# Cross-attention with layer normalisation on one core: the order of all engines listed anew, low parts of the projections last, half of the q copies on ScalarE and half of the scales on VectorE

## The chip, the cores and the metric

The kernel runs on one core of a Trainium2 chip. The metric is the device time in microseconds of one execution. The core has five engines, each of which runs its instructions strictly in program order: TensorE (PE in the profile, with PEld for its weight loads), VectorE (DVE), ScalarE (ACT), GpSimd (POOL) and SyncE (SP), which here issues DMA transfers. A matmul reads SBUF and writes PSUM, which has eight banks of 128 partitions x 512 fp32.

## The reference

```python
qs = (x @ wq).reshape(4, 2048, 16, 32).transpose(0, 2, 1, 3)
ks = (ctx @ wk).reshape(4, 77, 16, 32).transpose(0, 2, 1, 3)
vs = (ctx @ wv).reshape(4, 77, 16, 32).transpose(0, 2, 1, 3)
scores = einsum('bhqd,bhkd->bhqk', qs, ks) / sqrt(32)
scores = where(mask, -inf, scores)            # mask over the 77 keys
attn = einsum('bhqk,bhkd->bhqd', softmax(scores), vs)
out = attn.transpose(0, 2, 1, 3).reshape(4, 2048, 512) @ wo + x
mu, var = mean(out, -1), mean((out - mu) ** 2, -1)
return (out - mu) / sqrt(var + 1e-5) * gamma + beta
```

x is (4, 2048, 512) in fp32, ctx (4, 77, 512). There are 16 heads of 32 columns.

## The kernel before, in words

The 8192 rows of x form 64 tiles t of 128 rows, 32 blocks b of 256 rows (two tiles) and 16 groups g of 512 rows (four tiles). The accuracy of fp32 is kept in the two projections by splitting both operands into a high part in a short format and a low part, the remainder (`xth`/`xtl`, `wqh`/`wql`, `AH`/`AL`, `woh`/`wol`). Each projection is then a sum of three products, high by high, high by low and low by high, over four chunks c of 128: 12 matmuls of 128x512.

The order of all work is one long string, `ORDER`. It is a list of words, each a letter with a number: the letter names a step, the number its tile, block or group, and the program is written word by word, so the string fixes the order on each engine. The words that matter here:

- `Q` on PE: q projection of a group for four heads (12 matmuls, L275). Four of them fill the q of a group. `q` is the copy of the result out of PSUM (L289).
- `S` on PE: scores of a tile (64 small matmuls in 32x64 pieces, L405), four banks. `T` on DVE: mask added and row maximum taken (`pbuf`, `nm`, L422). `e` on ACT: the exponential (L437). `r` on DVE: the reciprocal of the sum (L447). `n` on POOL: the normalising product (L452). `t` on DVE: the transpose into `B` (L473).
- `P`: one of twelve DMA transfers of a block that regroup `B` into `PT` (L484). Its suffix gives the queue: `s` SyncE, `g` GpSimd, `a` ScalarE. `V` on PE: the product with the values (32 matmuls, L498), which needs all twelve. Where `V` stands right behind an `S` on PE, the first matmul of the `S` already waits for them.
- `a` on ACT and `b` on DVE: high and low part of the result (`AH` L527, `AL` L531). `O` on PE: out projection of a tile (12 matmuls, L554).
- `x`, `+`, `s`: x row tile loaded, residual added (DVE L563), moments (DVE L577, L578). `v` on POOL: 1/sqrt(var + eps) and -mean/sqrt(...) as four small operations (`rn`, L583 to L586). `k` on ACT: the scale with bias (L592). `f` and `)` on POOL: gain and shift (L595, L598). `w`: the store.
- `g`, `i`, `j`: x transposed loaded, cast to the high part (ACT), split into the low part (POOL L269).

A run of matmuls of one word is called a visit. A full visit is `Q`, `O` or another with 128 rows and columns, against `S` and `V`, which use the array in smaller pieces; a change of kind is where a visit of one of the three kinds follows one of another.

`SLOTS` assigns buffers and PSUM banks to the values in the order in which they come, so a new order goes with new numbers. Where VectorE splits wv or wo (`F`, `G`), the next `j`, `n`, `f` or `)` on POOL is made to wait until VectorE is done with it (`shared` and `wait_for`).

Of the kernel before, what the change touches and what calls it, by code (L numbers as in the profile page):

```python
# [8 lines left out]
F32 = mybir.dt.float32  # L9
# [25 lines left out]
for b in range(4):  # L35
# [7 lines left out]
NPB = 3  # L43
KSCALE = 1.0 / HD**0.5
# [10 lines left out]
T5.0 e6.1 P1.2s P1.1s P1.8s j7 Q14 Z16.s P1.6s n4 t4 S7 Z2.s T7.3 e5.2 e6.3 e6.2 e7.3 T7.0 e7.0 T7.2 T5.3 T5.1 r6
P1.11s T7.1 e7.1 e7.2 q14 P1.10s P1.9s P1.7s P1.4s Q8 q8 Q11 q11 r7 Q13 n6 t6 e5.3 e5.1 e5.0 S9 T9.0 n7 T9.3 t7 r5 n5
V1 a1.1 a1.0 b1.0 x0 g8 i8 j8 g9 b1.1 T9.1 V0 a0.1 T9.2 Z8.s b0.1 x3 Z15.s O2 L1 i9 x2 S8 P3.6s P3.2s P3.8s j9 t5 e9.1
a0.0 b0.0 e9.2 e9.0 +2 T8.3 e8.3 T8.1 e8.1 =24.8 T8.0 e8.0 s2 T8.2 O3 +3 s3 q13 v1 P3.10s Z14.s P3.0s O0 P3.7s P3.9s
P3.1s Z4.s P3.5s e9.3 S10 T10.2 +0 Y1 Z13.s P3.4s x4 T10.3 e8.2 P3.11s P2.7s P2.8s P3.3s T10.1 e10.3 r9 k3 e10.1 T10.0
e10.0 e10.2 r8 n8 f3 P2.5s P2.6s n9 )3 Z5.s P2.4s O1 +1 Q15 q15 s1 t8 Q12 q12 S11 T11.2 T11.1 e11.2 T11.3 e11.3 k2 V3  # L60
S12 a3.0 a3.1 s0 v0 k0 P2.1s P2.9s f2 r10 n10 t9 P2.10s P2.3s P2.11s P2.0s P2.2s g11 b3.0 T12.2 Z9.s w3 e11.1 e12.2
i11 j11 b3.1 Z11.s x7 f0 P4.0s P4.1s P4.9s P4.5s P4.8s g10 x5 P4.3s Q18 T12.1 q18 T12.0 T12.3 e12.3 T11.0 e11.0 P4.6s
x6 P4.4s O7 +7 S13 t10 s7 r11 n11 T13.2 T13.3 V2 a2.0 T13.0 P4.11s T13.1 P4.10s P4.7s P4.2s a2.1 b2.1 t11 P5.5s )2 k1
f1 Q19 O6 P5.3s P5.2s P5.10s P5.4s e12.0 S14 T14.1 T14.3 e12.1 r12 n12 T14.0 T14.2 b2.0 +6 s6 P5.9s w2 g12 e13.2 P5.0s
# [31 lines left out]
+26 S37 T37.2 T37.1 x29 T37.0 b14.0 P16.0s P16.9s f22 )22 e35.1 i22 e35.3 f23 )23 i23 r35 n35 j22 s27 V15 s26 v13 t35
T37.3 w22 P16.1s e36.0 x28 e37.1 e36.3 e36.2 P16.3s Q43 q43 e37.2 e37.0 a15.1 e37.3 r36 O29 k26 S38 T38.2 T38.0 T38.3
T38.1 e38.1 e38.0 P16.5s P17.1s P17.2s P17.6s O28 +29 +28 s28 s29 P17.7s g24 n36 r37 t36 j23 b15.1 a15.0 b15.0 v14
P17.0s f26 Q41 q41 n37 e38.2 P17.10s P17.8s P17.4s k27 w23 x31 k28 Q42 q42 S39 T39.2 P17.5s w25 T39.1 T39.3 e38.3 f27
k29 i24 P17.11s V16 a16.0 t37 j24 e39.3 r38 b16.0 n38 x30 P17.3s P17.9s S40 T40.3 T40.1 T39.0 e40.3 e39.1 P18.10s  # L100
P18.11s P18.8s P18.3s x32 P18.2s )26 P18.1s P18.6s P18.9s x33 O30 +30 s30 T40.0 O31 +31 t38 Q47 T40.2 a16.1 e39.0
e39.2 r39 n39 f28 s31 v15 b16.1 e40.2 e40.0 f29 )29 )28 S41 T41.3 e40.1 e41.3 T41.2 t39 V17 g25 T41.0 a17.1 T41.1
e41.2 L3 P18.4s P18.7s Q45 r40 w26 P18.5s b17.1 P18.0s P19.6s g27 n40 w28 P19.8s q47 Q44 q44 k31 f31 k30 f30 a17.0 i25
j25 S42 T42.1 P19.0s P19.1s P19.7s O33 e41.1 e41.0 )27 T42.0 T42.2 T42.3 e42.3 b17.0 O32 r41 +33 e42.0 s33 t40 S43 +32
e42.2 P19.9s P19.10s T43.2 P19.3s x34 w29 T43.0 P19.11s P19.2s T43.3 g26 x35 P19.5s P19.4s e42.1 T43.1 r42 n41 n42 s32
v16 t41 e43.3 V18 a18.0 a18.1 Q46 Q50 )31 =48.8 e43.1 e43.0 q46 q45 P20.5s i27 j27 P20.3s S44 P20.1s P20.9s x38 w27
q50 b18.0 P20.10s P20.7s T44.1 T44.0 x37 w31 T44.2 t42 O34 k33 T44.3 f33 e43.2 i26 k32 e44.0 e44.1 S45 T45.0 r43
# [67 lines left out]
def xattn_layernorm(  # L175
# [625 lines left out]
```

## Time and profile before

| | us |
|---|---|
| three runs | 508.16, 508.02, 506.6 |
| median of the runs | 508.02 |
| span of the profiled execution | 506.2 |
| the median less that span | 1.8 |

The profile comes from one execution; its span runs from the first to the last instruction. Engine rows give busy time, share of the span and number of instructions. In rows of groups stands: line, engine, operation, result <- operands by their names in the kernel, partitions x elements, type and count, then busy time and mean ns of one, then the idle time of the engine just before them with what ended it.

### The profile page before, as it was taken

The numbers are of one execution on the slowest core, as the hardware profiler recorded it, in microseconds if no ns is written. First come the engines' busy times: TensorE is split into PE (matmuls) and PEld (weight loads), VectorE is DVE, ScalarE is ACT, GpSimd is POOL, SyncE is SP. The second block draws the span as 40 slices with busy tenths as digits, with TensorE's granted clock in tenths as the row PEclk, the third lists the DMA queues.
The fourth block names the chain that finished last, engine by engine and source line by source line (L and its number), as shares of the span: only waits on it lengthen the run. The fifth ranks groups of instructions, "written<-read, shape, count | busy, mean of one in ns | idle before, by whom it ended". The sixth has DMA issues, their size and how long they took to land.

```text
span 506.2 us, 20312 instructions
## 1 busy us (share of the span) xinstructions
PE 498.8 (99%) x6831; PEld 383.1 (76%) x6831; DVE 460.5 (91%) x2539; ACT 473.9 (94%) x2248; POOL 421.3 (83%) x387
## 2 busy tenths in 40 slices
PE   9999999999999999999999999999999999999995
PEld 6987778777777777777777777777777777877773
DVE  5799988999899999898898898998999999899997
ACT  6699999999999999999999999999999998999851
POOL 2666464789886798989989887999998999999896
PEclk9999999999999999999999999999999999999999
DMA  8957577889886796859887778877888769888746
GB/s 306 396 197 175 135 212 183 221 210 217 247 242 178 177 248 199 249 165 253 243 216 204 200 207 240 230 201 193 248 232 225 207 177 293 247 199 222 183 150 232
DMA packets 58782, 110.86 MB, mean 219 GB/s; under 512 B 9462, under 2 KB 11278, under 8 KB 58678
## 3 DMA queue, kind: packets, MB, share of 16 engines
q1 hardware_dynamic: 54502, 101.30, 71.1%
q0 software_dynamic: 2496, 5.77, 4.0%
q10 hardware_dynamic: 1680, 2.49, 2.0%
q8 instruction: 54, 0.88, 0.8%
q14 instruction: 50, 0.41, 0.3%
HBM read 41.79 MB, written 16.78 MB: 116 GB/s over the span
## 4 chain that ended last, share of the span: by engine, by line
PE 98%; DMA 1%; DVE 1%; ACT 0%; issue 0%; DVEq 0%
PE po L554 36%; PE pq L275 35%; PE pa L498 11%; PE sc L405 11%; PE pv L326 2%; PE pk L299 1%; PE pq L685 1%; DMA stage_a<-kin 1%; PE pa L513 0%; DVE xtl L637 0%; PE po L543 0%; DVE st L606 0%; DVE po L634 0%; ACT woh L672 0%; DVE mvt L608 0%
## 5 line engine op out<-in xcount | busy, mean ns | idle before, releaser
L437 ACT ACTIVATE pbuf<-pbuf,nm 128x77 f32<-128x77 f32 x1024 | 353.0, 358 | 5.2 <-DVE nm L422 3.6
L437 ACT ACTIVATION_READ_ACCUMULATOR pbuf<-pbuf,nm 128x1 f32 x1024 | 203.2, 198 | 0.0
L422 DVE CUSTOM_DVE_ANT_0 pbuf<-sc,mb 128x77 f32<-128x77 f32 x1024 | 169.7, 231 | 7.4 <-PE sc L405 5.8
L452 POOL TENSOR_TENSOR pbuf<-pbuf,ri 128x1232 f32<-128x1232 f32 x63 | 142.2, 2258 | 36.7 <-DVE ri L447 25.4
L554 PE MATMUL po<-woh,AH 128*128 128x512 f32 x256 | 103.5, 404 | 0.0
L473 DVE STREAM_TRANSPOSE B<-pbuf 128x1280 f32<-128x1280 f32 x64 | 96.1, 1502 | 5.8 <-POOL pbuf L452 2.4
L275 PE MATMUL pq<-xth,wqh 128*128 128x512 f32 (+1 forms) x256 | 100.8, 394 | 0.2
L554 PE MATMUL po<-wol,AH 128*128 128x512 f32 x256 | 99.9, 390 | 0.0
L554 PE MATMUL po<-woh,AL 128*128 128x512 f32 x256 | 99.8, 390 | 0.0
L275 PE MATMUL pq<-xth,wql 128*128 128x512 f32 (+1 forms) x256 | 98.1, 383 | 0.0
L275 PE MATMUL pq<-xtl,wqh 128*128 128x512 f32 (+1 forms) x256 | 98.1, 383 | 0.0
L422 DVE DVE_READ_ACCUMULATOR2_ANT nm<- 128x1 f32 x1024 | 84.4, 82 | 0.0
L598 POOL TENSOR_TENSOR o<-o,bet 128x512 f32<-128x512 f32 x56 | 72.1, 1291 | 1.8
L595 POOL TENSOR_TENSOR o<-o,gam 128x512 f32<-128x512 f32 x56 | 72.2, 1293 | 0.1
L269 POOL TENSOR_TENSOR xtl<-xtf,xth 128x1024 fp32r<-128x1024 f32 x28 | 67.2, 2404 | 3.9 <-ACT xth L265 3.2
L405 PEld LDWEIGHTS sc<-kct,q 32*64 32x64 f32 x4096 | 51.4, 130 | 22.6 <-issue 12.2
L405 PE MATMUL sc<-kct,q 32*64 32x77 f32 x4096 | 61.2, 238 | 0.0
L498 PE MATMUL pa<-PT,vsb 96*32 96x256 f32 x992 | 59.7, 382 | 0.0
L554 PEld LDWEIGHTS po<-woh,AH 128*128 128x128 f32 x256 | 48.0, 188 | 14.3 <-issue 2.5
L275 PEld LDWEIGHTS pq<-xth,wqh 128*128 128x128 f32 x256 | 48.1, 188 | 13.7 <-DVE nm L422 1.2
L554 PEld LDWEIGHTS po<-woh,AL 128*128 128x128 f32 x256 | 48.1, 188 | 10.5 <-DVE AL L531 0.2
L275 PEld LDWEIGHTS pq<-xth,wql 128*128 128x128 f32 x256 | 48.1, 188 | 9.7
(108 smaller groups left out, 638.6 us busy)
## 6 DMA issues: line engine op xcount, KB each, us to landing
PT<-B SPq DMA_DIRECT2D x330, 128.0 KB
xtf<-xT SPq DMA_DIRECT2D x28, 512.0 KB
o<-x SPq DMA_DIRECT2D x56, 256.0 KB
out<-o SPq DMA_DIRECT2D x56, 256.0 KB
PT<-B POOLq DMA_DIRECT2D x25, 128.0 KB, 4.0
PT<-B ACTq DMA_DIRECT2D x17, 128.0 KB
stage_a<-kin SPq DMA_DIRECT2D x4, 410.0 KB
xtf<-xT SPq DMA_DIRECT2D x4, 256.0 KB
```

What stands on the lines that cost most here:

```text
L269: return nc.gpsimd.tensor_tensor(l[:, c : c + 2], fx.pop((g, c)), xh[g][:, c : c + 2].bitcast(F32), ALU.subtract)
L275: nc.tensor.matmul(pq, w[:, c, m * P : (m + 1) * P], r[g][:, c, rs], start=(n == 0), stop=(n == 11))
L326: nc.tensor.matmul(pv[: rows.stop - rows.start], ctx_s[c][i][:, rows], v[c], start=(n == 0), stop=(n == 11))
L405: mm = nc.tensor.matmul(sc[j][r0 : r0 + SR, g * NK : (g + 1) * NK], qs[q, g, rs.start + r0 : rs.start + r0 + SR], kct[q, g, t // TPB, keys ...
L422: nc.vector.tensor_tensor_reduce(pb[:, h // 2, (h % 2) * NK : (h % 2 + 1) * NK], scs[t][j][:, g * NK : (g + 1) * NK], mb[:, t % TPB, keys_ ...
L437: nc.scalar.activation(pb[:, h // 2, (h % 2) * NK : (h % 2 + 1) * NK], pb[:, h // 2, (h % 2) * NK : (h % 2 + 1) * NK], AF.Exp, bias=nmax[t ...
L452: return nc.gpsimd.tensor_tensor(pv, pv, rv.to_broadcast((P, NP, 2, NK)), ALU.mult)
L473: nc.vector.transpose(bt.rearrange("p c q r -> p q c r"), pbuf[t % NPB].rearrange("p q (c r) -> p q c r", c=5),)
L498: nc.tensor.matmul(pas[b, g // 2][HD * j : HD * (j + 1), (g % 2) * BLK : (g % 2 + 1) * BLK], vsb[:, 2 * b // TPB, h % 2, HD * (h // 2) : H ...
L554: nc.tensor.matmul(pos[t], a[:, c, rs], w[:, c, :], start=(first and c == 0 and n == 0), stop=(c == NC_D - 1 and n == 2),)
L595: return nc.gpsimd.tensor_tensor(od[t], od[t], gam, ALU.mult)
L598: return nc.gpsimd.tensor_tensor(od[t], od[t], bet, ALU.add)
```

## The change

The string is listed anew from its 36th word on, for all engines, and `SLOTS` with it. A change of kind on PE comes 144 times instead of 150. The other parts:

- `hi_then_lo`: both projections run high x high and low weights x high (q), or the like for the out projection, for all four chunks, and then the four products with the low operand.
- A second number in `Q` and `O` words (`Q28.11`, `O15.3`) is a count of no-ops that `pad` spreads between the matmuls of the visit: 384 in all, at most two behind one matmul.
- `q` with the suffix `.1` (30 of 60) copies on ACT instead of DVE.
- `k` with the suffix `.1` (32 of 56) scales on DVE, as (o - mean) x rn. Such tiles are in `CENTRED`; where both tiles of a block are (11 blocks), `rsqrt` leaves out two of its four operations. The next `j`, `n`, `f`, `)` or `v` on POOL waits for such a scale, as it does for `F` and `G`.
- The regroupings stand in other places. Of the 372 `P` words 330 have the suffix `s`, 25 `g` and 17 `a`, as before. The new switches `by_scalar` of the loads and `IN_PSUM` are not used by a word of the list.

```diff
+def hi_then_lo(wh, wl, hi, lo):
+    return [(w, hi, c) for c in range(NC_D) for w in (wh, wl)] + [(wh, lo, c) for c in range(NC_D)]
...
 ORDER = """
...
-e21.3 P9.3s s12 v6 j15 b7.1 e22.2 Q26 x14 q26 t20 Q27 q27 r21 n21 S23 T23.3 T23.0 T23.1 g16 P9.1s e22.3 r22 V8 a8.1
-O17 S26 T26.3 j17 e24.3 k15 T26.0 T25.2 P10.8s P10.4s r24 n24 V9 P10.7s P10.2s T26.1 k14 P10.0s w10 P10.6s P10.5s w13
...
+Q25.4 e21.3 r20 v6 P8.10s j15 s10 T22.1 P8.4s P8.5s a7.1 e21.1 a7.0 e21.0 O11.2 e22.1 T22.0 P8.3s b7.1 Q26.1 +11 k12
+k13 x14 r21 P8.7s n20 P9.1s T22.3 s11 w8 q25 P9.5s q26 e22.2 V8 P9.6s S23 v5 a8.0 n21 f12 b7.0 P9.9s O14 P9.11s t20
+a9.1 e25.2 T26.0 T26.3 T25.0 P11.10s e25.1 +17 P11.1s b9.0 e25.0 )10 g19 e25.3 Q29 k15 q29.1 Q31 P11.6s b9.1 n24 k14.1
...
+CENTRED = {int(w[1:].split(".")[0]) for w in ORDER.split() if w[0] == "k" and "." in w}
...
+    def pad(n, nops):
+        for _ in range((n + 1) * nops // 12 - n * nops // 12):
+            nc.tensor.nop(hint="pad")
...
-        for c in range(NC_D):
-            for w, r in ((wqh, xh), (wqh, xl), (wql, xh)):
-                nc.tensor.matmul(pq, w[:, c, m * P : (m + 1) * P], r[g][:, c, rs], start=(n == 0), stop=(n == 11))
+        for w, r, c in hi_then_lo(wqh, wql, xh, xl):
+            nc.tensor.matmul(pq, w[:, c, m * P : (m + 1) * P], r[g][:, c, rs], start=(n == 0), stop=(n == 11))
+            pad(n, nops)
...
-            nc.vector.tensor_copy(once(qd, g, [P, NG, GRP], F32, "q")[:, m, :], pq)
+            copy = nc.scalar.copy if by_scalar else nc.vector.tensor_copy
+            copy(once(qd, g, [P, NG, GRP], F32, "q")[:, m, :], pq)
...
-        for c in range(NC_D):
-            for n, (a, w) in enumerate(((ah, woh), (ah, wol), (al, woh))):
...
+        for n, (w, a, c) in enumerate(hi_then_lo(woh, wol, ah, al)):
+            nc.tensor.matmul(pos[t], a[:, c, rs], w[:, c, :], start=(first and n == 0), stop=(n == 11))
+            pad(n, nops)
...
-        nc.gpsimd.tensor_tensor(rn[:, 1, :], mv[:, :, 0], rn[:, 0, :], ALU.mult)
-        nc.gpsimd.tensor_tensor(rn[:, 1, :], rn[:, 1, :], mneg, ALU.mult)
+        if not {2 * b, 2 * b + 1} <= CENTRED:
+            nc.gpsimd.tensor_tensor(rn[:, 1, :], mv[:, :, 0], rn[:, 0, :], ALU.mult)
+            nc.gpsimd.tensor_tensor(rn[:, 1, :], rn[:, 1, :], mneg, ALU.mult)
...
+        if t in CENTRED:
+            mean = mvs[t // 2][:, tt, 0:1]
+            return nc.vector.tensor_scalar(o, pos.pop(t, o), mean, rn[:, 0, tt : tt + 1], ALU.subtract, ALU.mult)
...
-            if op in "FG":
+            if op in "FG" or op == "k" and k and int(k) in CENTRED - IN_PSUM:
                 shared = ins
-            elif shared and op in "jnf)":
+            elif shared and op in "jnf)v":
```

First place, TensorE at the values product of block 9 (`pa`; `sc` are scores, `pq` a q projection). Before:

```order
L405 MATMUL sc_2_3557<-kct,q_2739 64x77
L405 MATMUL sc_3_3558<-kct,q_2739 64x77
L498 MATMUL pa_0_3616<-PT_3003,vsb 32x256 x8
L498 MATMUL pa_1_3617<-PT_3003,vsb 32x256 x8
L275 MATMUL pq_0_3707<-xth_2833,wqh 128x512
L275 MATMUL pq_0_3707<-xtl_3051,wqh 128x512
L275 MATMUL pq_0_3707<-xth_2833,wql 128x512
```

And after:

```order
L420 MATMUL sc_2_3547<-kct,q_2886 64x77
L420 MATMUL sc_3_3548<-kct,q_2886 64x77
L513 MATMUL pa_0_3582<-PT_3221,vsb 32x256 x8
L513 MATMUL pa_1_3583<-PT_3221,vsb 32x256 x8
L420 MATMUL sc_0_3618<-kct,q_2886 64x77
L420 MATMUL sc_1_3619<-kct,q_2886 64x77
```

Behind the values product a full visit stood before; now another tile's scores do.

Second place, TensorE in one q visit (the third of group 1, early in the program). It shows the order of the products and a no-op. After:

```order
L288 MATMUL pq_2_699<-xth_329,wqh 128x512
L288 MATMUL pq_2_699<-xth_329,wql 128x512
L288 MATMUL pq_2_699<-xth_329,wqh 128x512
L288 MATMUL pq_2_699<-xth_329,wql 128x512
L288 MATMUL pq_2_699<-xth_329,wqh 128x512
L288 MATMUL pq_2_699<-xth_329,wql 128x512
L288 MATMUL pq_2_699<-xth_329,wqh 128x512
L288 MATMUL pq_2_699<-xth_329,wql 128x512
L288 MATMUL pq_2_699<-xtl_371,wqh 128x512 x4
L283 NO_OP
```

Before, `xtl` was the operand of every third matmul, as in the `pq_0_3707` rows above; now of the last four.

Third place, VectorE at the low part of block 9 (`AL`). Before:

```order
L577 BN_STATS st_3688<-o_3499 128x6
L578 BN_AGGR mv_3668<-st_3688 128x2
L531 TENSOR_TENSOR AL_3656<-pa_0_3616,AH_3654 128x512
L289 COPY q_3404<-pq_0_3707 128x512
L289 COPY q_3404<-pq_3_3721 128x512
L447 RECIPROCAL ri_3737<-sum_3487 128x16
```

And after:

```order
L546 TENSOR_TENSOR AL_3734<-pa_0_3582,AH_3692 128x512
L546 TENSOR_TENSOR AL_3734<-pa_1_3583,AH_3692 128x512
L607 TENSOR_SCALAR o_3215<-o_3215,mv_3403,rn_3696 128x512
L437 ISA pbuf_82,nm_3713<-sc_1_3619,mb_1611 128x77
L437 ISA nm_3713 128x1
```

The q copies behind it are gone from VectorE, and the scale of tile 14 (`o_3215`) stands there, ahead of the maxima of tile 26.

GpSimd in the same stretch of the new order:

```order
L467 TENSOR_TENSOR pbuf_80<-pbuf_80,ri_3704 128x8x154
L614 TENSOR_TENSOR o_3052<-o_3052,bet 128x512
L614 TENSOR_TENSOR o_2961<-o_2961,bet 128x512
L594 TENSOR_TENSOR rn_3870<-mv_3656,small 128x2
L595 TENSOR_TENSOR rn_3870<-rn_3870,small 128x2
L611 TENSOR_TENSOR o_3215<-o_3215,gam 128x512
L467 TENSOR_TENSOR pbuf_81<-pbuf_81,ri_3831 128x8x154
```

The first row is `n24`, ahead of the scale of tile 14 in the list; the second, `)11`, is the operation that waits for that scale. Block 8 has both tiles in `CENTRED`, so two small operations of its `v` stand here instead of four.

More of the change, by code (lines that the diff above doesn't have):

```diff
@@ L55 @@
[L55 to L64, printed above, removed]
@@ L96 @@
[L96 to L105, printed above, removed]
@@ new lines @@
+P15.7s x26 n33 S35 Q40 t33 T35.1 e34.0 P15.0s P15.10s P16.8s O27.7 T35.0 b14.1 P16.1s )22 P16.7s P15.9s T35.3 q40.1
+T35.2 v12 e35.1 j23 P15.4s P16.10s P16.0s e35.0 P16.3s e35.3 f23 P16.11s )23 a14.0 S36 O26.1 T36.2 e34.1 w23 T36.1 x30
+T36.0 )21 T36.3 +27 j22 k24.1 +26 w22 e35.2 f24 b14.0 w21 r34 s27 n34 s26 V15 x28 S37 e36.2 k25.1 e36.1 r35 t34 e36.3
+O28 O29.1 x33 P16.4s T37.2 P16.2s v13 T37.1 T37.0 a15.1 k26 Q42.3 +28 a15.0 f25 n35 e36.0 e37.1 f26 T37.3 e37.2 L3
+e37.0 b15.1 r36 q42.1 )24 g24 t35 S38 T38.0 b15.0 )26 x29 +29 e37.3 P16.5s k27.1 T38.1 T38.3 s28 O30.1 e38.1 Q43.2
@@ new lines @@
+Q44.1 b17.0 x32 e41.2 e41.0 P18.0s )29 r40 n40 P18.9s w24 S42 P19.7s T42.2 P19.10s T42.3 O33.3 b17.1 e41.1 P18.1s
+T42.0 )31 P19.4s t40 e41.3 )28 P19.2s P19.11s f30 g26 P19.6s P19.9s T42.1 r41 O32.4 e42.0 q44.1 e42.1 w29 S43 +32 +33
+w28 V18 x37 T43.0 e42.3 e42.2 T43.2 T43.1 i27 P19.3s a18.0 n41 S44 P19.0s T43.3 t41 P19.8s s33 a18.1 T44.2 j27 r42 n42
+O35 s32 P19.5s P19.1s P20.11s e43.0 P20.7s =56.8 b18.0 v16 x34 i26 T44.0 e43.1 Q49.6 O34 b18.1 +35 q49.1 e44.0 e43.2
+e43.3 k33.1 k32.1 T44.3 P20.8s s35 t42 T44.1 j26 V19 S45 e44.3 r43 Q48 T45.1 T45.2 e45.1 w31 x38 x36 P20.4s f32 n43
@@ new lines @@
+t52 )43 f42 Q57.6 q57 )45 S55 x46 V24 b23.1 P25.9s w39 w43 e54.0 T55.2 e54.2 f44 )44 T55.0 x48 e54.3 x47 r54 T55.3 t53
+P25.5s P26.3s S56 P25.6s a24.0 e55.0 T56.3 T55.1 w44 e55.3 O46.1 P26.10g Q60.14 T56.1 e55.2 e55.1 O47.3 T56.0 b24.0
+w45 x57 P26.0s n54 P26.4g a24.1 +46 s46 T56.2 P26.9a e56.3 q60.1 r55 e56.0 b24.1 P26.11s n55 x60 e56.1 P26.6g P26.5s
+t54 S57 V25 +47 e56.2 )42 T57.2 T57.0 x49 T57.1 x50 e57.2 P26.7g P26.2a S58 a25.1 r56 t55 P26.8g n56 O48 e57.0 P27.4a
+T58.1 s47 P27.9s P26.1s P27.10g T58.2 T58.0 T57.3 O49.3 e57.1 e58.2 +48 b25.1 v23 w42 Q63 P27.8g k47.1 a25.0 +49 e57.3
@@ new lines @@
+T61.2 w48 T62.3 )49 e61.3 b27.1 e61.2 e62.3 s50 T62.1 P29.5s P29.7g T62.2 O52.17 n60 V28 T62.0 x54 e62.0 P29.1g a28.0
+r61 w46 +52 x63 a28.1 n61 e62.2 S63 P29.11a P29.3g P29.2s v25 t60 e62.1 T63.1 O54.4 b28.0 k50 t61 P29.8s P29.0g T63.2
+x56 w49 e63.2 P30.5g +53 b28.1 r62 P30.8s f50 s53 s52 T63.0 P30.3g n62 P30.7s P30.9s T63.3 e63.1 e63.0 O57 e63.3
+O56.18 P30.11s V29 x55 P30.0s P30.1s v26 t62 h63.0 U62.6s a29.0 k51 )50 +54 a29.1 O55.13 m63.0 P30.4s h63.1 P30.2a
+m63.1 P30.10s P30.6s U62.7s &57 f51 ~57 b29.0 U62.8a U62.2s &56 U62.11s b29.1 t63 u57 y57 U62.10a U63.9a k53.1 U63.2s
@@ L146 @@
+IN_PSUM = {int(w[1:].split(".")[0]) for w in ORDER.split() if w[0] == "k" and w.endswith(".2")}
 SLOTS = {
     "mm": (
-        "5012367450123456702315467023614372546310642574032165070153462705627345064723517024635120462314507614"
-        "2304312567025341025430167234501453701274301560147325614530716354027146325410637250463421573064213075"
-        "1320764137601264710267045312604123576201746217450632471427635142367052065732410637247652043102653706"
-        "2534705632015436205461720302176203651724631250467315462753406127034207364512063742103747063217453162"
@@ L153 @@
+        "4210567356043157613254075246047356102643570325164705163072"
     ),
@@ L551, in o_proj @@
             pos[t] = bank(f"po_{t}")
-        for c in range(NC_D):
-            for n, (a, w) in enumerate(((ah, woh), (ah, wol), (al, woh))):
-                nc.tensor.matmul(
-                    pos[t],
-                    a[:, c, rs],
-                    w[:, c, :],
-                    start=(first and c == 0 and n == 0),
-                    stop=(c == NC_D - 1 and n == 2),
-                )
+        for n, (w, a, c) in enumerate(hi_then_lo(woh, wol, ah, al)):
+            nc.tensor.matmul(pos[t], a[:, c, rs], w[:, c, :], start=(first and n == 0), stop=(n == 11))
+            pad(n, nops)
     def residual(t):
+        if t in IN_PSUM:
+            return residual_psum(t)
         nc.vector.tensor_tensor(od[t], pos.pop(t), od[t], ALU.add)
@@ L721, in xattn_layernorm @@
         "c": lambda k, part: av_hi(k // 2, k % 2, True), "d": lambda k, part: av_lo(k // 2, k % 2, True),
-        "x": lambda k, part: load_x(k), "X": lambda k, part: resid(k), "O": lambda k, part: o_proj(k),
+        "x": lambda k, part: load_x(k, part), "X": lambda k, part: resid(k), "O": lambda k, part: o_proj(k, part),
         "+": lambda k, part: residual(k), "&": lambda k, part: residual_psum(k),
@@ L739, in xattn_layernorm @@
             ins = ops[op](int(k or 0), int(part or 0))
-            if op in "FG":
+            if op in "FG" or op == "k" and k and int(k) in CENTRED - IN_PSUM:
                 shared = ins
-            elif shared and op in "jnf)":
-                wait_for(ins, shared, "VectorE's pass over two tiles of SBUF is begun ahead of GpSimd's")
+            elif shared and op in "jnf)v":
+                wait_for(ins, shared, "VectorE's pass over both of its ports is begun ahead of GpSimd's")
                 shared = None
```

193 lines of the change are left out of this document (99 added, 94 removed).

## The prediction

> **What bounds the kernel now.** I read the page first: engine shares, then the chain that ended last.
>
> ```profile
> PE 498.8 (99%) x6831; PEld 383.1 (76%) x6831; DVE 460.5 (91%) x2539; ACT 473.9 (94%) x2248; POOL 421.3 (83%) x387
> PE 98%; DMA 1%; DVE 1%; ACT 0%; issue 0%; DVEq 0%
> ```
>
> TensorE works for 498.8 of 506.2 us and is 98% of the chain. ACT and DVE are near full too, so TensorE sets the time only while they keep up. Then the waits of TensorE (line, releaser: us in total, times, longest), of its matmuls and of its weight loads, and the busy time of each engine from the first q projection to the last visit:
>
> ```profile
> PE pw L648 <- PEq L792: 0.8, 1, 0.8
> PE pk L299 <- ACT woh L672: 0.3, 1, 0.3
> PEld sc L405 <- DVE nm L422: 5.1, 13, 0.4
> core 0: us, PE busy (x) PEld busy (x) DVE busy (x) ACT busy (x) POOL busy (x), PEclk, DMA share, GB/s
> 17.90:499.80 481.90, 481.72 (x6728) 369.15 (x6726) 445.08 (x2509) 463.02 (x2225) 411.97 (x365) 1.00 0.78 215
> ```
>
> The matmuls wait twice, both ahead of 17.9 us. A weight load for scores waits 13 times for the row maxima of VectorE, by 0.4 us at most: behind the matmul in flight, but a sign that in 13 of 64 score visits a PSUM bank came free just in time. In these 481.90 us DVE has 36.8 us to spare, ACT 18.9, POOL 69.9; the granted clock is 1.00. So the time is the sum of the visits, and what a visit costs depends on its neighbours. TensorE's timeline shows that (start, duration; a visit's length is from its first start to that of the next visit):
>
> ```profile
> 201.69 0.39 PE L275 MATMUL pq<-xth,wql 128*128 128x512 f32 x1
> 201.91 0.39 PE L275 MATMUL pq<-xth,wqh 128*128 128x512 f32 x1
> ...
> 204.41 0.39 PE L275 MATMUL pq<-xth,wql 128*128 128x512 f32 x1
> 204.72 0.95 PE L405 MATMUL sc<-kct,q 32*64 32x77 f32 x64
> 205.61 1.93 PE L498 MATMUL pa<-PT,vsb 96*32 96x256 f32 x32
> 207.47 0.95 PE L405 MATMUL sc<-kct,q 32*64 32x77 f32 x64
> 208.35 0.50 PE L554 MATMUL po<-woh,AH 128*128 128x512 f32 x1
> 208.69 0.39 PE L554 MATMUL po<-wol,AH 128*128 128x512 f32 x1
> ...
> 211.19 0.39 PE L275 MATMUL pq<-xth,wqh 128*128 128x512 f32 x1
> ...
> 213.91 0.39 PE L554 MATMUL po<-woh,AH 128*128 128x512 f32 x1
> ...
> 217.61 1.93 PE L498 MATMUL pa<-PT,vsb 96*32 96x256 f32 x32
> 219.47 0.50 PE L554 MATMUL po<-woh,AH 128*128 128x512 f32 x1
> ...
> 222.35 0.39 PE L554 MATMUL po<-woh,AH 128*128 128x512 f32 x1
> ```
>
> A full visit (12 matmuls of 128x512) between full visits takes 2.72 (211.19 to 213.91), 0.22 to 0.23 a matmul. Ahead of scores its last matmul has 0.31 instead (204.41 to 204.72): +0.08. Behind scores a full visit takes 2.84 (208.35 to 211.19): +0.12; the slowest of this kind:
>
> ```profile
> 94.71 0.50 PE L275 MATMUL pq<-xth,wqh 128*128 128x512 f32 x1
> ...
> 97.59 0.39 PE L554 MATMUL po<-woh,AH 128*128 128x512 f32 x1
> ```
>
> 2.88: +0.16. Behind values it takes 2.88 (219.47 to 222.35): +0.16. Scores take 0.88 to 0.89 ahead of either kind, values 1.86.
>
> **The change, part by part.** Every term is a change to the profiled execution, whose span is 506.2; the median of the runs is 508.02, so 1.8 lie around the span.
>
> *Kinds on TensorE.* Counted from the tables of words: full visits with another kind behind them go from 57 to 52, full visits behind scores from 41 to 48, full visits behind values from 16 to 4. (The matmuls stay 12, 64 and 32 a visit.) At the prices above: -5 x 0.08 = -0.4; +7 x 0.13 = +0.9 (nearer to the common 2.84 than to 2.88); -12 x 0.16 = -1.9. Sum -1.4. That values lead into scores 27 times instead of 15 costs nothing by 205.61 to 207.47; two scores in a row go from 2 to 3, at most some 0.1, taken as 0. [...]
>
> *Low parts last.* The same 12 matmuls a visit. The low operand is due at the ninth instead of the second (q) or third (out): 7 and 6 x 0.227 = 1.6 and 1.4 us later. Only what waits now can gain: the weight loads for out projections waited for the low part once,
>
> ```profile
>   DVE AL L531: 0.2, 1
> ```
>
> so 0. What covers it if wrong: nothing needs the earlier order.
>
> *No-ops, 384, at most two a matmul.* No row shows one. The dearest sequencer instruction is the first row below; the cheapest bound is the scores visit above, where 64 loads and 64 matmuls are issued in 0.88 us, 7 ns each.
>
> ```profile
> L554 PEldq EVENT_SEMAPHORE  x29: 51/51/51, 70.9 to 492.7; - x29
> ```
>
> Two at 51 ns are 0.10 within a spacing of 0.227, so the matmul in the array hides them: 0. Unhidden they would be 384 x 0.051 = 19.6, or 2.7 at 7 ns; below nothing only if a pause shortened the slow spacing behind scores (fourth rival).
>
> *q copies and scales.* The rows that carry it (busy us, mean ns):
>
> ```profile
> L289 DVE COPY q<-pq 128x512 f32<-128x512 f32 x60 | 40.0, 674 | 5.7 <-PE pq L275 5.7
> L385 DVE TENSOR_SCALAR mb<-m 128x1536 bf16<-128x1536 uint8 x1 | 1.0, 952 | 0.0
> L671 DVE CAST ctx_h<-stage_a 128x308 fp32r<-128x308 f32 x1 | 0.3, 321 | 4.4 <-DMA stage_a<-kin 4.4
> L367 DVE TENSOR_TENSOR wol<-stage_b,woh 128x512 fp32r<-128x512 f32 x4 | 2.8, 708 | 0.0
> L592 ACT ACTIVATE o<-o,rn 128x512 f32<-128x512 f32 x56 | 44.2, 817 | 1.5 <-POOL mvt L619 1.2 <-POOL rn L586 0.3
> L527 ACT CAST AH<-pa 128x512 fp32r<-128x512 f32 x64 | 35.8, 580 | 4.5 <-PE pa L498 2.9 <-PE pa L513 0.7 <-ACT pbuf L437 0.4
> ```
>
> DVE loses 30 copies: -30 x 0.674 = -20.2. It gains 32 scales of 128x512 from SBUF to SBUF, an operation that the trace lacks: between the cast of 308 and the tensor_scalar of 1536 columns a column costs (952 - 321) / 1228 = 0.514 ns, so 321 + 204 x 0.514 = 0.43 each; at most the 0.71 of L367. I take 0.43, the row of the same instruction: +13.8 (to 22.7). DVE goes to 438.7 (to 447.6) of 481.9. ACT: -32 x 0.817 = -26.1, and 30 copies from PSUM at the 0.580 of L527, +17.4: 454.3. Both lie beside TensorE, which by the waits shown hung on DVE only in places. One such place cost time, a score visit of 1.08 instead of 0.88:
>
> ```profile
> 255.08 1.15 PE L405 MATMUL sc<-kct,q 32*64 32x77 f32 x64
> 256.16 0.50 PE L275 MATMUL pq<-xth,wqh 128*128 128x512 f32 x1
> ```
>
> I count -0.2 for it, as DVE is given 6.4 us more air. If ACT is late with a q copy, the score visits of that group wait: they stand behind all four copies.
>
> *GpSimd.* 22 small operations go (195 ns each by L585 below): -4.3, hidden. Its next operation behind each DVE scale now waits for that scale: at most 32 x 0.43 = 13.8 of 69.9 idle us, and what is queued behind it is normalising, on which the transposes wait; 0 by its spare time.
>
> *Regroupings.* 330 of 372 words are on SP before and after, so the queues are as they were. Their places move: in ten blocks the last one now stands within one visit ahead of the values product. Taken as 0, since the queue issues when the transposed weights are there, not when TensorE passes; price below.
>
> *Tail* (behind 499.8, 6.4 us): same words, 0.
>
> Sum: -1.4 - 0.2 = -1.6: a span of 504.6, a time of 506.4. Against 508.02, 0.3% (1.5 us, about what a measurement of this kernel tells from no change) puts the bounds at 506.5 and 509.5.
>
> **Rivals.**
>
> First, slower: *a DVE scale is held by a GpSimd operation in flight.* Evidence, VectorE's split of the weights and GpSimd's split of x:
>
> ```profile
> L355 DVE TENSOR_TENSOR wvlAH<-stage_b,wvh x2: 685/687/689, 26.2 to 30.7; 128x512 fp32r<-128x512 f32 x2
> 34.32 0.90 DVE L355 TENSOR_TENSOR wvlAL<-stage_b,wvh 128x512 fp32r<-128x512 f32 x1
> 32.25 2.42 POOL L269 TENSOR_TENSOR xtl<-xtf,xth 128x1024 fp32r<-128x1024 f32 x1 [0.68 <-issue]
> L585 POOL TENSOR_TENSOR rn<-mv,rn 128x2 f32<-128x2 f32 x28 | 5.5, 195 | 2.2
> L595 POOL TENSOR_TENSOR o<-o,gam 128x512 f32<-128x512 f32 x56 | 72.2, 1293 | 0.1
> L269 POOL TENSOR_TENSOR xtl<-xtf,xth 128x1024 fp32r<-128x1024 f32 x28 | 67.2, 2404 | 3.9 <-ACT xth L265 3.2 <-issue 0.7
> ```
>
> At 34.32 the same subtraction took 0.90 instead of 0.687, while GpSimd ran to 34.67. Many scales in the new order stand right behind a GpSimd operation. Half of an operation of 1.29 to 2.40 is some 0.95; GpSimd is busy 85%: 32 x 0.85 x 0.95 = 26 us more on DVE, 465 of 481.9. Where a fifth of it reaches TensorE (13 of 64 score visits just in time), +5.2: 511.6. It decides from four holds of 0.8 that reach TensorE (506.4 + 3.2 > 509.5). Against it: the row shows +0.2, not the half of an operation, and the next GpSimd operation waits. Chance 0.18. [...]
>
> Second, slower: *a regrouping lands late.*
>
> ```profile
> DMA to landing us min/median/max: 1.9/3.9/6.9
> ```
>
> If the issue waits until its place, 3.9 against a visit of 2.7 is 1.2 late, ten times 12; in three of ten, +3.6: 510.0. Chance 0.09.
>
> Third, no change: visits behind scores at 2.88 throughout (48 x 0.03 = +1.4) or thin spots on ACT and DVE: 507.8. Chance 0.15.
>
> Fourth, more gained: with pauses and late low parts the visits behind scores lose their slow spacing, 2.80 instead of 2.85: -48 x 0.05 = -2.4: 504.0. Nothing in the profile shows it. Chance 0.13.
>
> That the change doesn't do all it names (the queues of the regroupings) touches no term.
>
> **How the numbers follow.** The likeliest case, 0.45: 506.4, own range 505.0 to 507.8, of which 0.33 lies below 506.5 and 0.12 above. Faster: 0.33 + 0.13 = 0.46. Same: 0.12 + 0.15 = 0.27. Slower: 0.18 + 0.09 = 0.27. The range goes from the fourth rival's 504.0 less the rest to 503.8, up to the first rival's price, 511.5; beyond lie about half of that rival and the worse half of the second.
>
> **What would show it.** TensorE still 98% or more of the span; full visits behind values at 2.88 only four times; padded visits at 2.72 (NOPs wrong if 2.8 or more); mean of the DVE scale near 430 ns (first rival: 800 or more, and waits of scores for nm grow in count); q copies on ACT near 580; no wait of pa for PT (second rival). I am wrong if the score visits lengthen past 0.9 in more than a few places.

## The result, and the profile after

The changed kernel takes 513.43 us (median of 4 runs, 510.67 to 513.83) against 507.87 for the kernel before on the same chip: a ratio of 1.0102, interval 1.0075 to 1.0129. In six later runs it took 513.90 (1.0123, 1.0096 to 1.0151). Slower by 5.6 us, where a gain of 1.6 had been forecast.

First the page: engine shares and the chain that ended last.

```profile
PE 499.9 (98%) x6831; PEld 384.8 (75%) x6831; DVE 458.0 (89%) x2541; ACT 466.7 (91%) x2246; POOL 417.3 (82%) x365
POOL 11%; DVE 8%; DMA 6%; PE 5%; SPq 2%; issue 1%; ACT 0%; ACTq 0%; POOLq 0%; DVEq 0%
```

TensorE works as long as before (499.9 against 498.8), DVE and ACT 2.5 and 7.2 us less, but the chain that was 98% TensorE now runs over GpSimd, VectorE and transfers. The waits of TensorE's matmuls and of its loads for scores:

```profile
PE pa L513 <- DMA PT<-B: 1.8, 1, 1.8
PE sc L420 <- DMA PT<-B: 1.7, 1, 1.7
PE sc L420 <- DVE nm L437: 0.2, 1, 0.2
PEld sc L420 <- DVE nm L437: 5.9, 15, 0.4
```

The engines' busy time from the first q projection to the last visit:

```profile
18.02:504.90 486.88, 482.62 (x6728) 370.59 (x6726) 442.08 (x2511) 455.87 (x2223) 407.56 (x342) 1.00 0.77 213
```

Two regroupings came too late for TensorE. The first place is the values product of block 2, in the timeline:

```profile
96.91 1.07 PE L288 MATMUL pq<-xtl,wqh 128*128 128x512 f32 x4
99.80 2.57 PE L513 MATMUL pa<-PT,vsb 96*32 96x256 f32 x32 [1.81 <-DMA PT<-B]
102.29 1.42 PE L420 MATMUL sc<-kct,q 32*64 32x77 f32 x64
103.64 0.80 PE L568 MATMUL po<-woh,AH 128*128 128x512 f32 x1
```

The windows over the same stretch (the granted clock is the third number from the end):

```profile
97.00:99.80 2.80, 0.98 (x6) 0.51 (x5) 0.66 (x2) 2.58 (x10) 2.80 (x2) 1.00 0.81 212
99.80:102.30 2.50, 2.50 (x34) 1.23 (x34) 2.46 (x13) 2.50 (x17) 0.31 (x1) 0.73 0.91 271
102.30:103.70 1.40, 1.40 (x68) 1.24 (x65) 1.40 (x11) 1.40 (x10) 0.38 (x1) 0.50 1.03 250
```

The wait is 1.81 us, and behind it the clock is granted at 0.73 and 0.50 in the two windows (1.00 up to 100.95, 0.50 from there to 104.36): the values take 2.49 instead of 1.86, the next scores 1.35 instead of 0.88. The place costs 3.3 in all, with the wait and what is left of the slow clock in the visit behind.

The second place is the scores that wait with the values of block 22; with what follows it costs 2.35, at a clock of 1.00:

```profile
388.63 1.05 PE L420 MATMUL sc<-kct,q 32*64 32x77 f32 x64 [1.65 <-DMA PT<-B]
389.62 1.93 PE L513 MATMUL pa<-PT,vsb 96*32 96x256 f32 x32
392.07 0.89 PE L420 MATMUL sc<-kct,q 32*64 32x77 f32 x58 [0.23 <-DVE nm L437]
```

I added up the visits of both traces, each at the median for its kind and neighbours: from the first to the last visit 481.92 became 486.88, which is -1.3 from the kinds and +6.3 of waits and slow matmuls. Of these some 5.7 are the two places; some 0.8 are short waits in scores behind values (tiles 28, 30, 32, 33, 45), and the rest is scatter of single visits, in both directions. A tail 0.7 longer and a start 0.1 later make up the 5.8 by which the span grew, 506.2 to 512.0.

### The profile page after: what moved, and what is told of

Read it like the earlier page. It is cut to its first block, busy times and chain, and to the rows that moved or that the text cites. A ratio compares the mean times of both kernels' runs of the same rounds, so it can differ in the third digit from the quotient of the medians.

```text
span 512.0 us, 20690 instructions
## 1 busy us (share of the span) xinstructions
PE 499.9 (98%) x6831; PEld 384.8 (75%) x6831; DVE 458.0 (89%) x2541; ACT 466.7 (91%) x2246; POOL 417.3 (82%) x365
## 3 DMA queue, kind: packets, MB, share of 16 engines
q10 hardware_dynamic: 1680, 2.49, 1.8%
## 5 line engine op out<-in xcount | busy, mean ns | idle before, releaser
L568 PE MATMUL po<-woh,AL 128*128 128x512 f32 x256 | 68.6, 390 | 0.0
L288 PE MATMUL pq<-xtl,wqh 128*128 128x512 f32 (+1 forms) x256 | 66.7, 382 | 0.0
L568 PEld LDWEIGHTS po<-wol,AH 128*128 128x128 f32 x256 | 48.2, 188 | 9.3 <-issue 0.2
## 6 DMA issues: line engine op xcount, KB each, us to landing
xtf<-xT SPq DMA_DIRECT2D x28, 512.0 KB
```

Of the source, the lines that this page charges most:

```text
L288: nc.tensor.matmul(pq, w[:, c, m * P : (m + 1) * P], r[g][:, c, rs], start=(n == 0), stop=(n == 11))
L568: nc.tensor.matmul(pos[t], a[:, c, rs], w[:, c, :], start=(first and n == 0), stop=(n == 11))
```

## Experiments

In each, the time of the kernel before is that of the same chip. Order edits are told in words, since the strings are long.

**1. Two repairs in SyncE's order.** The last regroupings of blocks 22 and 2 go out earlier; the edit for block 22:

```diff
-... x41 Q53.2 P23.2s k39.1 ... P23.1s ... P23.3s ... P22.3s ... P22.1s ... P22.2s ... S51
+... x41 Q53.2 P22.3s k39.1 ... P22.1s ... P22.2s ... P23.2s ... P23.1s ... P23.3s ... S51
```

> The changed kernel with two repairs in SyncE's order alone: the last three regroupings of block 22 trade places with the first three of block 23, and the last two of block 2 are issued ahead of an x load, with two loads of value rows moved behind. Theory A (two late regroupings): the holes ahead of V2 (1.9 us) and of S51 (1.7 us), with the slow clock behind them (1.5 and 0.6), vanish: 513.4 - 5.7 = 507.7, range 506.5 to 509. Rival B (the transfer engines are overloaded, so lateness only moves on to another block): two other holes of 1 to 2 us, 511 or more. Rival C (GpSimd's waits for the scales delay the stores, and these SyncE): the hole of block 22 stays, 511.

511.59 us (before 507.49; 1.0084, 1.0063 to 1.0105): 1.8 gained, not 5.7. The place at block 22 is gone, that at block 2 half:

```profile
PE pa L513 <- DMA PT<-B: 1.0, 1, 1.0
PE po L568 <- DVE AL L546: 0.4, 1, 0.4
```

but other waits came out that the holes had covered: 0.58 in the scores of tile 14 and 1.1 in the out projections of tiles 29 and 30, on VectorE's low parts. Theory A was right on the place and wrong on what it is worth. The time is the one that rival B named, and a part of its mechanism shows: the counter on which SyncE's transfers report their landing, in 16 steps each, puts the last landing of block 2 at 5.1 us behind its issue in the changed kernel and at 6.7 here, so that going out 2.5 earlier won only half. The waits at tiles 14, 29 and 30, though, hang on VectorE.

**2. One regrouping made late in the kernel before.**

```diff
-P22.7s O40 P23.6s ... P23.1s P23.4s t48 x45 Q52
+P23.4s O40 P23.6s ... P23.1s P22.7s t48 x45 Q52
```

> The kernel before with one exchange: a regrouping of block 22 and one of block 23 change places, so that block 22's last goes out at 381.2 to 381.8 us (by the trace of before) instead of 373.2, 2.3 us ahead of the scores that wait with the values product of block 22. Theory A: it lands 3.9 us after its issue, so a hole of some 1.6 us ahead of S51 and slow matmuls behind it worth 0.6: 507.5 + 2.2 = 509.7, range 508.5 to 511. Rival: a transfer of 2.3 us or less, or other slack, hides it: 507.5.

513.75 (before 507.85; 1.0117, 1.0095 to 1.0139): 5.9 us for one transfer.

```profile
387.54 1.03 PE L405 MATMUL sc<-kct,q 32*64 32x77 f32 x64 [3.44 <-DMA o<-x]
```

The window behind it, with the granted clock third from the end:

```profile
387.50:391.70 4.20, 4.17 (x99) 2.29 (x99) 4.19 (x24) 1.24 (x7) 0.81 (x1) 0.67 0.34 129
```

The regrouping's issue ran from 380.23 to 381.27, and by the 16 steps of its counter it landed at 387.29, just ahead of the scores at 387.54: 7.1 us, not the 3.9 that the expectation took. (The profile names the x load issued behind it, whose last step came at 388.14, too late to have ended the wait.) With a clock of 0.67 behind it the place costs 5.2. In the kernel before, the same transfer took 6.9, but had gone out 11.8 us ahead of its product. So the mechanism is shown in both directions: a regrouping made late makes TensorE wait here, and made earlier it frees the place (block 22 in experiment 1).

**3. Low parts last alone**, in the kernel before (`hi_then_lo` in both projections).

> The kernel before with one part alone: both projections do the four products with the low operand last. Theory A: no change, 507.9 within 1.5, full visits 2.72 between full visits and 2.84 to 2.88 behind scores. Rival: the order of the products itself sets the slow spacing behind scores: 41 visits 0.05 shorter or longer, 505.8 or 510.

507.80 against 507.49 (1.0006, 0.9996 to 1.0017): nothing, as forecast.

**4. No no-ops.** The suffixes of `Q` and `O` words are taken off.

> The changed kernel without its 384 no-ops, all else as it is. Theory A: they are hidden, 513.4 within 1.5. Rival D: they cost what a sequencer instruction costs, 7 to 51 ns each: 2.7 to 19.6 us faster, 494 to 510.7. Rival E: they shorten the slow spacing behind scores, and without them it is 1 to 2 us slower.

516.44 (1.0212, 1.0168 to 1.0256): 3 us slower than with them, which no theory had by this amount. A stall stands inside one visit, behind the 57th of 64 matmuls, and nothing in the profile released it:

```profile
240.02 1.05 PE L419 MATMUL sc<-kct,q 32*64 32x77 f32 x57
242.17 0.36 PE L419 MATMUL sc<-kct,q 32*64 32x77 f32 x7 [1.09 <-issue]
```

By the transfer records the instruction queue's nearest transfer ended 1.40 us ahead of the restart. So the new theory H: TensorE's own code came late. The visit is 1.6 us longer for it. Two late regroupings with waits of 1.9 and 1.3 us, at other places than with the no-ops, stand beside it.

**5. 24 no-ops early**, none elsewhere (`Q4.24`), to move that edge by a known amount.

> The changed kernel without its no-ops but for 24 of them, all in the second q visit (two behind each matmul). Theory H (without no-ops TensorE's own instructions come late: its code is loaded in pieces, and the piece's edge falls into the scores of tile 32, where two kernels without no-ops stood still behind matmul 56 or 57 of 64): with 24 instructions more ahead of it the same edge falls 24 instructions, 12 pairs of load and matmul, earlier: a stall behind matmul 44 or 45 of tile 32, again 1.4 us behind the end of a transfer on the instruction queue; time 514 to 518. Rival (the stall is a late operand or bank): still behind matmul 56, or gone.

516.44 (1.0172, 1.0132 to 1.0213), and the stall stands where H put it, behind matmul 45; the transfer ended 1.27 us ahead of the restart.

```profile
241.33 0.78 PE L419 MATMUL sc<-kct,q 32*64 32x77 f32 x45
244.16 0.48 PE L419 MATMUL sc<-kct,q 32*64 32x77 f32 x19 [2.04 <-issue]
```

A second stall of the kind, in an out projection at 336.60, ended 1.30 us behind such a transfer:

```profile
PE po L567 <- issue: 1.1, 1, 1.1
```

Counted in TensorE's records, matmuls and loads, the first stall stands at the same number in experiments 4, 5 and 9, about 6850, and this one 2560 records later. A run without the padding has 54 transfers of 16 KB on the instruction queue for some 13,900 records, which is some 257 a transfer, so that ten lie between the two stalls (an estimate from these counts). The stall moved with the count of instructions, as H has it: an edge of TensorE's code falls into tile 32's scores without padding, and a piece can come late there; most edges show no stall. The price of one no-op was rightly 0; what the no-ops place was not seen.

**6. No wait of GpSimd for the scales.**

```diff
-            if op in "FG" or op == "k" and k and int(k) in CENTRED - IN_PSUM:
+            if op in "FG":
...
-            elif shared and op in "jnf)v":
+            elif shared and op in "jnf)":
```

> The changed kernel without the wait of GpSimd's next operation for a scale on VectorE. Theory A: GpSimd's idle time ahead of gains that wait for a scale (11.9 us) shrinks only where the gain itself needs no scale, the mean scale grows from 611 ns to some 700 to 1000, the holes of V2 and S51 stay: 513.4 within 1.5. Rival C (the waits delay stores and with them SyncE): the hole of block 22 goes, 2 to 3 us faster. First rival of the prediction (a scale held by GpSimd): mean scale 1.3 us or more, 32 x 0.7 = 22 us on VectorE, 3 to 5 us slower.

522.68 (1.0280, 1.0251 to 1.0310): 9.3 slower than the changed kernel. The scale (ns min/median/max) in the changed kernel:

```profile
L607 DVE TENSOR_SCALAR o<-o,mv,rn x32: 455/540/1600, 94.6 to 488.2; 128x512 f32<-128x512 f32 x32
```

And without the wait:

```profile
L607 DVE TENSOR_SCALAR o<-o,mv,rn x32: 455/545/4099, 94.2 to 498.0; 128x512 f32<-128x512 f32 x32
```

TensorE's waits there:

```profile
PE sc L420 <- DVE nm L437: 3.2, 9, 0.9
```

In sum 19.2 and 28.2 us: VectorE's scales take 9.0 us more, the kernel 9.3. The longest, of 4.1 us, runs beside GpSimd for 3.8 of them. The first rival's mechanism is real, and the wait holds it down. The kernel loses about as much as VectorE does, not a fifth; how much of that is waits and how much the slow clock behind them (0.62 and 0.64 behind two of them) isn't told apart. The hole of block 22 stays (1.7 us), so the rival by which GpSimd's wait for the scales delays the stores fails.

**7. The swap without the order.** The changed code, 30 q copies on ScalarE and 32 scales on VectorE, in the order of before, no no-ops; then each half alone.

```diff
-q15 s1 t8 Q12 q12 S11 T11.2 T11.1 e11.2 T11.3 e11.3 k2
+q15.1 s1 t8 Q12 q12 S11 T11.2 T11.1 e11.2 T11.3 e11.3 k2.1
```

> The changed code (low parts last, the same 30 q copies on ScalarE, the same 32 scales on VectorE with GpSimd's wait) in the order and with the buffers of before, without no-ops. Theory A (the order costs, not the swap): 507.5 within 1.5. Rival F (a scale held by GpSimd's operation in flight costs by itself, in any order): scales of 0.6 to 1.0 us mean, and TensorE waits for nm of some us: 510 to 515.

> The order of before with low parts last and only the q half of the swap: 30 q copies on ScalarE in their old places. In the trace with both halves ScalarE waited 14.9 us in 8 copies for a projection still running, with exponentials behind it. Theory (an engine in order pays for the place, not for the sum): 520 to 540, most of the 41 us. Rival: the scales were the larger part, 509 to 516.

> The order of before with low parts last and only the other half of the swap: 32 scales on VectorE in their old places, with GpSimd's wait for them. Theory: VectorE waits 4 us for the rsqrt, the scales take 0.87 us on average, GpSimd waits 16 us for them: 512 to 525, the smaller part of the 41 us. Rival (first rival of the prediction as the whole cause): 530 or more.

548.65 with both (1.0797, 1.0774 to 1.0821), far beyond both expectations, 540.03 with the q half (1.0628, 1.0610 to 1.0645), 549.61 with the scales (1.0827, 1.0811 to 1.0842). I had taken the q half for nearly all and the scales for the smaller part; each alone is dear, and they don't add. A half alone also moves work to one side only (ACT 488.9 us busy with the q half, DVE 483.8 with the scales), so only the run with both (468.8 and 468.2) tests the places without a fuller engine. ScalarE's waits with the q half:

```profile
ACT q L302 <- PE pq L286: 14.0, 7, 4.0
```

Those of GpSimd and TensorE with the scales:

```profile
POOL pbuf L465 <- DVE o L605: 8.8, 2, 5.1
POOL o L612 <- DVE o L605: 8.1, 2, 7.7
PE sc L418 <- DVE nm L435: 7.4, 8, 4.6
```

The reading is that an engine in order pays for the place of an instruction: a copy that waits for its projection holds the exponentials behind it, a gain that waits for a scale holds the next normalising. With the scales alone they took 455 to 2532 ns, so a scale held by GpSimd is a part of it too; the runs do not split the 41 us.

**8. The order without half of the swap.** The new order with all scales on ScalarE again.

> The changed kernel with all 56 scales on ScalarE again, in the places of the new order; 30 q copies stay on ScalarE. Theory A (the swap fits the new order, it is not the loss): ScalarE gets 32 x 0.82 = 26 us more, 493 of 512, and TensorE waits: 516 to 530. Rival F (scales on VectorE, held by GpSimd, are the loss): faster, 508 to 511.

533.89 (1.0526, 1.0497 to 1.0555): 20 slower than the changed kernel. ScalarE is busy 488.7 us here against 466.7, so its load is a part of this. The new order needs the scales on VectorE, and experiment 7 shows that the swap needs a new order.

**9. SyncE's whole queue by due time**, without and with the no-ops taken off, and a second try with a flaw mended.

> The changed kernel with SyncE's queue alone put in a new order, from block 2's regroupings to block 30's: each transfer goes out as early as its data allow, the one due first ahead (regroupings due 7.5 us ahead of their values product, x loads 6.5 us ahead of the residual). The other engines keep their order. Worked out from the times of the changed kernel's trace, the last regrouping of a block is then issued a median of 13 us ahead of its product instead of 7. Theory A (SyncE's order makes the lateness): nearly all of the 6.3 us of TensorE waits goes but some 0.8 ahead of scores: 513.4 - 5.5 = 508, range 506.5 to 509.5. Rival B (transfers are limited by the engines that move them): 511 or more. Rival F (VectorE and GpSimd are late by themselves, by held scales): waits on VectorE stay, 510 to 512.

> As the kernel with SyncE by due time, but without the 384 no-ops. If the no-ops only shift when transfers fall due (the 3 us that they were worth in the changed kernel were late regroupings): within 1 of that kernel. If they shift where TensorE's own code is loaded (a stall of 1.1 us inside the scores of tile 32, put down to no releaser): 1 to 2 us slower than that kernel, with such a stall in the trace.

> SyncE's queue by due time once more, with the flaw of the first try mended: loads of x transposed keep their old times, and an x load goes out no sooner than 4.5 us behind the store that frees its buffer, so that it does not hold up the queue. In the first try a load of x transposed landed 4.7 us late for ScalarE, and 5 us of waits hung on that. Theory A (queue order makes the lateness): no wait for a regrouping, and none of that kind on ScalarE: 508.5 to 510.5, what is left being VectorE's lateness of 2 to 3 us. Rival G (any repair of one queue uncovers the next, nothing is won): 511 or more.

517.51 (1.0182, 1.0158 to 1.0206), 521.74 (1.0273, 1.0238 to 1.0308) and 516.10 (1.0169, 1.0153 to 1.0184): all slower than the changed kernel. No matmul waits for a regrouping any more in the first and the third, but a load of x transposed of 512 KB came late for ScalarE (third kernel; then TensorE's longest waits there):

```profile
ACT xth L275 <- DMA xtf<-xT: 7.3, 3, 4.9
PE sc L420 <- DVE AL L546: 1.9, 2, 1.6
PE sc L420 <- ACT q L304: 1.8, 1, 1.8
```

Casts, q copies and high parts stand behind it on ScalarE, and the place costs 6.0 us. In the second kernel the stall in tile 32's scores is back, behind matmul 56, 1.36 us behind the end of the instruction transfer, as H says:

```profile
253.87 0.53 PE L419 MATMUL sc<-kct,q 32*64 32x77 f32 x8 [2.82 <-issue]
```

**10. The two places of that trace mended** (the load of x transposed and three x loads go out earlier).

> The second try at SyncE's queue with the two places mended that its trace still shows: the load of x transposed that ScalarE waited 4.9 us for (6.0 us of TensorE's time at tiles 21 and 12) goes out two regroupings and an x load earlier, and the x loads of tiles 4, 6 and 0 go out 3 to 7 us earlier (VectorE waited 2.7 us for the last, 1.4 us of TensorE's time at tile 13). Theory A (the losses are separate late transfers, each with its place): 516.1 - 7.4 = 508.7, up to 510 where VectorE's lateness comes out instead. Rival G (a repair uncovers the next wait): 512 or more.

514.76 (1.0126, 1.0109 to 1.0143), not 508.7: tile 21's 4.2 shrank to 1.8, but tile 14 and a q visit ahead of it wait 2.8. Rival G was nearer.

**11. VectorE relieved.** Its 32 scales work on 8 of 512 columns, in the kernels of experiments 1, 9 and 10.

```diff
+            o = o[:, :8]
-            return nc.vector.tensor_scalar(o, pos.pop(t, o), mean, rn[:, 0, tt : tt + 1], ALU.subtract, ALU.mult)
+            return nc.vector.tensor_scalar(o, o, mean, rn[:, 0, tt : tt + 1], ALU.subtract, ALU.mult)
```

> The kernel with the two repairs in SyncE's order, and VectorE relieved: its 32 scales are done on 8 of 512 columns only (the rest of those rows is left unscaled), in the same places. Theory A' (behind the late regroupings the next limit is VectorE, which is late with maxima and low parts in the new order): the waits left in that kernel's trace (tiles 13, 14, 28, 30, 32, 45 and out projections 29 and 30, 3 us in all) shrink by most of it: 511.6 - 2.5 = 509. Rival (what is left are late transfers): 511 to 512, the waits stay.

> The same with the 32 scales of VectorE done on 8 of 512 columns only (the rest of those rows is left unscaled). Theory A + A' (late transfers and VectorE's lateness are the whole of the loss): 507 to 508.5, about the 1.3 us of the changes of kind below the sum of the visits of before plus a longer tail of 0.7. Rival G: 510 or more, the waits move to ScalarE or GpSimd.

> The same with the 32 scales of VectorE on 8 of 512 columns only (the rest of those rows is left unscaled). Theory A + A': 507 to 508.5. Rival G: 511 or more.

510.73 (1.0052, 1.0034 to 1.0070), 515.02 (1.0138, 1.0115 to 1.0160) and 510.67 (1.0054, 1.0036 to 1.0072): 0.9, 1.1 and 4.1 better than with whole scales. The intervals of the first two overlap with those of the kernels with whole scales, so that only the last gain is clear of the noise; none of the three came down to what theory A' forecast. The waits on low parts at tiles 29 and 30 go from 1.1 and 1.0 to 0 and 0.2 in the first and the last. VectorE's lateness is part of the loss; even without it the order stays 2.6 to 2.8 us above the kernel before in the best two. The trace of the first still has late transfers at three values products; that of the last (its fastest run, 509.46) has none. Its two long visits are the scores of tile 14, 1.0 us longer, and those of tile 21, which wait for ScalarE:

```profile
PE sc L420 <- ACT q L304: 1.6, 1, 1.6
```

**12. The changed kernel once more**, for a second trace.

> The changed kernel once more, as it is, for a second profiled execution. If the late places are fixed by the order, the two holes (values of block 2, scores ahead of the values of block 22) stand at the same places with 1 to 2 us each, and the small waits of tiles 28, 30, 32, 45; if transfers merely scatter, other places. Time 511 to 514.

513.90. The places stand again, with smaller waits: 0.6 us at block 2 (the last row; its regrouping landed 0.2 us ahead of the product, though the profile names VectorE) and 1.0 at block 22. One of 1.1 us at block 30's values is new:

```profile
PE pa L513 <- DMA PT<-B: 1.1, 1, 1.1
PE sc L420 <- DMA PT<-B: 1.0, 1, 1.0
PE pa L513 <- DVE o L574: 0.6, 1, 0.6
```

In these two traces the order sets where TensorE can wait, and the landing of the transfers how long.

## Why the prediction was wrong, point by point

*Kinds on TensorE: right.* The visits at their medians came out 1.3 shorter (forecast 1.4).

*Low parts last: right* (experiment 3). *No-ops: right as a price, wrong as a whole*: full visits stay at 2.72, but without the no-ops TensorE stands still in tile 32's scores for 1.1, 2.0 and 2.8 us (4, 5, 9), by theory H because a piece of its code comes late. Taking them off costs 3 us between the medians; the stall itself is 1.6 of that in experiment 4's trace, and the rest isn't taken apart.

*Swap of copies and scales: the copy's size was right, the scale's too small, the conclusion wrong.* The groups in the trace:

```profile
L304 ACT COPY q<-pq 128x512 f32<-128x512 f32 x30 | 17.5, 582 | 2.8 <-PE pq L288 2.8
L607 DVE TENSOR_SCALAR o<-o,mv,rn 128x512 f32<-128x512 f32 x32 | 19.2, 611 | 1.2 <-POOL rn L595 1.1
```

The copy was put at 580; the scale at 430 (least measured 455, mean 611 with the holds). But "both lie beside TensorE" took a sum of busy times for slack. In experiment 7 the same swap in the old order costs 41 us, though ACT and DVE are busy for no more than 468.8 of 544.7.

*First rival: the mechanism there, its share wrong.* With GpSimd's wait the longest scale is 1.6 us, and the mean of 611 lies under the 800 that was to show this rival. Without it, in experiment 6, the longest is 4.1 us, 3.8 of them beside GpSimd. A fifth was to reach TensorE; there the kernel lost as much as VectorE (9.3 and 9.0 us).

*Third and fourth rival: neither.* Full visits between scores and another full visit stayed at 2.84 at the median, neither 2.88 nor 2.80. The thin spots on VectorE that the third also named did show, as a loss.

*Regroupings: the step that failed.* They were "taken as 0, since the queue issues when the transposed weights are there, not when TensorE passes". In the trace it doesn't: in the new order other words stand ahead. Block 22's last went out at 384.75, 23 us behind the end of its transpose, and SyncE stood still for 6.2 us on the way (363.6 to 369.8), ahead of a store whose row GpSimd had not finished. The waits of SyncE's queue for GpSimd's shift in the whole run (us in total, times, longest), after:

```profile
SPq L617 <- POOL o L614: 16.7, 5, 6.2
```

And before:

```profile
SPq L601 <- POOL o L598: 20.1, 11, 3.1
```

No run takes that one wait away, so its share in the delay is not shown. The last regrouping of a block goes out a median of 7.7 us ahead of the first matmul that waits for it, against 10.9 before (blocks 3 to 29, from the issue times in both traces).

Landing got hardly slower on SyncE's queue. The row that the prediction read, 1.9/3.9/6.9, and the same row after rest on 31 of the 396 regroupings alone, those of GpSimd's queue behind 407 us:

```profile
DMA to landing us min/median/max: 2.7/4.7/7.2
```

For SyncE's, the steps of their counters give a median of 3.7 us before and 3.8 after, an estimate from the 341 and 342 transfers whose steps are nearly all in the trace. Block 22's last landed in 3.8: it was late only because it went out late. Block 2's took 5.1. The second rival named this place but priced a late one at 1.2: it cost 3.3 and 2.4 here, 5.2 in experiment 2's trace, since single landings are longer than the median, and, at two of the three, for the slow clock behind the wait. At this price its chance of 0.09 was too small.

*The waits: -0.2 became +6.3.* The deeper fault is that the sum had no term for slack. In the old order the profile shows no matmul that waits between 17.9 and 499.8 us. The new one has nearly the same work on every engine, but less room on SyncE, VectorE and ScalarE, and in every repair other waits came out (1, 9, 10, 11). What stays open is how the 2.6 to 2.8 us left in experiment 11 divide over all runs; no version here beat the kernel before.

## What to carry to other kernels

Where the bounding engine never waits, a new order can gain only the small change in its own sequence (-1.3 us here) and can lose at every feeding queue (+6.3): price for each queue how long ahead of its use the last transfer or copy is issued, against the worst landing time and not the median (7.1 us in experiment 2 against some 3.7), and look at which transfers a landing row rests on. A wait that reaches TensorE costs itself and can cost a slow clock behind it (1.81 and 3.44 us did, 1.65 did not). Moving work between two engines that run in order is judged by what waits behind each moved instruction, not by the change in busy time (41 us lost in experiment 7, with ACT and DVE busy for 468.8 us of 544.7 at most).

## What the runs showed of the hardware that I had not expected

- TensorE stood still inside a dense run of small matmuls (experiments 4, 5, 9) and once in a full visit (5), and nothing in the profile released it: stalls of 1.1 to 2.8 us, ended 1.3 to 1.4 us behind a transfer of the instruction queue, the first moved by 12 matmuls with 24 no-ops. The reading is that it ran out of instructions.
- A wait of 1.81 us, up to 99.80, was followed by a granted clock of 0.50 from 100.95 to 104.36; one of 1.65 us was followed by 1.00.
- A tensor_scalar on 128x512 fp32 in SBUF took 455 ns at least and, in experiment 6, up to 4.1 us, 3.8 of them beside GpSimd.
- A regrouping of 128 KB on SyncE's queue lands in some 3.7 us at the median (an estimate from counter steps), but the one that experiment 2 made late took 7.1; of its 16 steps the first came at 3.9 us.
